# The int8 cross attention of a four-layer kernel, rewritten as a pipeline by ticks with engines in fixed order

## The chip, the cores and the metric

The kernel runs on one core of one Trainium2 chip. Its engines are TensorE (PE, with its weight loads shown as PEld), VectorE (DVE), ScalarE (ACT), GpSimd (POOL) and SyncE (SP), which issues most DMAs. The metric is the device time of one execution in microseconds; the median of several runs is given. A profile is one more execution, recorded by the hardware profiler.

## The reference, cut to what matters

The program computes four residual layers over x of 4 x 512 x 512: a cross attention with int8 fake quantisation, a mixture of experts, a second cross attention and a feed-forward. Only the first is touched. With 16 heads of 32 columns:

```python
def _qdq(x):
    s = jnp.maximum(jnp.max(jnp.abs(x), axis=-1, keepdims=True) / 127.0, 1e-08)
    return jnp.clip(jnp.round(x / s), -127.0, 127.0) * s
q = _qdq(x) @ _qdq(wq).T + bq
kv = cond @ wkv.T + bkv
k, v = jnp.split(kv, 2, axis=-1)          # then split into 16 heads
attn = jax.nn.softmax(jnp.einsum('bnhd,bmhd->bhnm', q, k) * scale, axis=-1)
o = jnp.einsum('bhnm,bmhd->bnhd', attn, v).reshape(B, N, C)
out = _qdq(o) @ _qdq(wp).T + bp

x = x + jnp.tanh(g_xattn[0]) * _L0_xattn_ref(_layernorm(x, axis=-1), ctx_2048, ...)
```

## The kernel before, in words

`xattn_int8` is the first stage. For each of 4 batches it goes through 4 groups of 4 heads (`oc`); a group is a unit of 16 score tiles, four heads by four tiles of 128 queries, each tile 128 queries by 512 keys. There are 256 score tiles in all.

For a score tile, `scores` multiplies query and key (PE, L438), takes the negated row maximum (DVE, L443) and the exponential with its row sums (ACT, L446). `turn`, two ticks later, transposes the tile in four pieces (PE, L460) and copies it from PSUM to the tile `a_pT` (`evac`, alternately DVE L120 and ACT L122). `weigh`, after every eight tiles, makes 16 small products with the values (PE, L468), each with 32 output columns, so that four heads stand beside each other in PSUM, and copies the result to `a_oT`. When a batch's four groups are done, `codes` turns 128 tokens back, divides by the sums and rounds them to int8 codes; `project` turns the codes, multiplies by `wp` (PE, L505), scales (DVE, L510), adds the bias (POOL, L511) and adds to x (DVE, L513).

The preparation of a batch (`prepare`) makes the values (PE L373, DVE L377), the layer norm and codes of x (L137 to L159), their turning (L382) and a row of scales (L165, L166). That of a unit (`heads`) makes the key (L403) and the query (L414, L419). `stacked` splits each into a high and a low half (ACT L334, DVE L335), so that a product of 4 x 32 rows sums high and low parts. It writes both halves to DRAM in one transfer (L339) and reads them back in four (L342), each of which fills 32 partitions for all four heads.

A product of plain f32 operands, as in L403, L373 and L468, stands in the trace as two matmul instructions with a weight load each; those of f32r (L438) and bf16 (L414, L505), and the transposes, as one.

The order comes from two places. `Line` puts steps behind each other: steps that are due in a tick, then `ceil(rest / ticks left)` preparation steps, each of which is a whole block of several engines' instructions (L199 to L205). The framework's scheduler may then reorder instructions between engines by their readiness. `Ordered` and `Beat` stand further down the file: `Ordered` keeps an engine's instructions in the order in which the program gives them (its calls all show as L567), `Beat` sorts steps by tick and by named place in the tick. The mixture of experts and the second attention use them already.

All PSUM is held by four pools of two banks each: `ps_m` for preparation and projection, `ps_s` for scores, `ps_t` for transposes, `ps_o` for weighing. `clear_slots` (L265) fills 39 slots in DRAM with zeros, which the mixture of experts needs later; it has the scheduler put them behind the loading of the next context.

Of the kernel before, what the change touches and what calls it, by code (L numbers as in the profile page):

```python
# [22 lines left out]
P = 128  # L23
# [46 lines left out]
class Kernel:  # L70
# [27 lines left out]
    def load_x(self, b):  # L98
        xv = self.a["x"].rearrange("(n p) d -> p n d", p=P)
        self.nc.sync.dma_start(self.x[:, ts(b, TB), :], xv[:, ts(b, TB), :])  # L100

# [7 lines left out]

    def spread(self, pool, name):  # L110

        v = pool.tile([P, D], F32, name=f"{name}_sb")
        self.nc.sync.dma_start(v, self.a[name].partition_broadcast(P))
        return v
# [70 lines left out]
class Line:  # L185

    def __init__(self):
        self.now, self.due, self.steps, self.ticks = 0, {}, [], 1  # L190

    def later(self, ticks, step):
        self.due.setdefault(self.now + ticks, []).append(step)

    def fill(self, steps, ticks):

        self.steps, self.ticks = list(steps), ticks

    def tick(self):  # L199
        for step in self.due.pop(self.now, []):  # L200
            step()
        for _ in range(-(-len(self.steps) // max(1, self.ticks))):
            self.steps.pop(0)()
        self.ticks -= 1
        self.now += 1  # L205

    def fill_all(self):
        while self.steps:
            self.steps.pop(0)()

    def drain(self):
        while self.due:
            self.tick()


def xattn_int8(k):

    nc, tc, a = k.nc, k.tc, k.a
    HG = KC
    with ExitStack() as ctx:
        wpool = ctx.enter_context(tc.tile_pool(name="a_w", bufs=1))
        p1 = ctx.enter_context(tc.tile_pool(name="a_1", bufs=1))
        p2 = ctx.enter_context(tc.tile_pool(name="a_2", bufs=2))
        p4 = ctx.enter_context(tc.tile_pool(name="a_4", bufs=4))
        p5 = ctx.enter_context(tc.tile_pool(name="a_5", bufs=5))  # L230
        p6 = ctx.enter_context(tc.tile_pool(name="a_6", bufs=6))
        dram = ctx.enter_context(
            tc.tile_pool(name="a_d", bufs=2, space=bass.MemoryType.DRAM)
        )
        ps_m = ctx.enter_context(tc.tile_pool(name="a_psm", bufs=2, space=PSUM))
        ps_s = ctx.enter_context(tc.tile_pool(name="a_pss", bufs=2, space=PSUM))
        ps_t = ctx.enter_context(tc.tile_pool(name="a_pst", bufs=2, space=PSUM))
        ps_o = ctx.enter_context(tc.tile_pool(name="a_pso", bufs=2, space=PSUM))
        scale = 1.0 / math.sqrt(DH0)

        wkvT = wpool.tile([P, KC, 2 * D], F32, name="wkvT")
        wkv = a["wkvT"].rearrange("(c p) o -> p c o", p=P)
        ctxTs = {}

        def load_ctx(b, chunks=((0, KC),)):
            ctxTs[b] = p1.tile([P, KC, S], F32, tag="a_ctxT", name=f"a_ctxT{b}")
            of = a["ctxT"][:, ts(b, S)].rearrange("(c p) t -> p c t", p=P)
            for c0, c1 in chunks:
                got = nc.sync.dma_start(ctxTs[b][:, c0:c1], of[:, c0:c1])
                if b == 0:  # L250
                    nc.sync.dma_start(wkvT[:, c0:c1, D : 2 * D], wkv[:, c0:c1, D : 2 * D])
            return got.ins


        load_ctx(0, [(c, c + 1) for c in range(KC)])
        bv = k.spread(wpool, "bv")
# [6 lines left out]
        def clear_slots(n, m, behind):  # L263
# [9 lines left out]
                ),  # L273
                reason="not needed early",
            )

        def coded_weight(name):


# [1752 lines left out]
```

## Time and profile before

| What | Value |
|---|---|
| median of 3 runs | 3576.08 us (3575.98 to 3579.71) |
| profiled execution, its own time | 3574.1 us |
| its span, first to last instruction | 3572.4 us |
| busy share of the span | PE 93%, DVE 61%, ACT 43%, POOL 38% |
| mean granted TensorE clock | 0.970 |
| first score of the first stage (L438) | at 61.7 us |
| last exponential of the first stage (L446) | at 602 us |
| last addition to x of the first stage (L513) | at 628.3 us |

A row of the groups or of the timeline names the line of the kernel, the engine and the operation, then the tiles as out<-in, the shape, and how many. Behind a bar or in brackets stands the idle time of the engine just before, and what ended it. A row of the waits reads: who waited, for whom, microseconds in total, how many times, the longest. Busy time of PE is a poor measure of its fullness, since matmuls are pipelined and the ends shown are modelled; the distance from one weight load to the next says more.

### The profile page before, as it was taken

What the parts mean: (1) busy time and instruction counts of PE and PEld (TensorE: products, weight loads), DVE (VectorE), ACT (ScalarE), POOL (GpSimd) and SP (SyncE); (2) the same over time, 40 slices, a digit from 0 to 9 for tenths busy, and PEclk for the clock granted to TensorE, in tenths of its full rate; (3) what the DMA queues carried; (4) which work ended last, traced back from release to release, by engine and by line L of the source; (5) the groups of instructions that cost most, each with busy time, mean ns of one, the idle gap of its engine ahead of it and who ended that gap; (6) DMA issues with size and microseconds to landing.
All of it is one profiled execution on the core that took longest, in us unless ns stands there. A gap on an engine that the chain in (4) does not pass through costs nothing.

```text
span 3572.4 us, 47015 instructions
## 1 busy us (share of the span) xinstructions
PE 3333.4 (93%) x15536; PEld 2190.3 (61%) x15552; DVE 2172.4 (61%) x4580; ACT 1544.1 (43%) x4456; POOL 1355.3 (38%) x1526
## 2 busy tenths in 40 slices
PE   6988987889999889989999999999999999999997
PEld 3544544534554444447777777776777777777775
DVE  6676767543133336525558766678766687676657
ACT  2544545111211223345554455554555554555543
POOL 1000000341000134624446654557545466544443
PEclk8999999899999999989999999999999999999998
DMA  5534441476354673552323233223332332333211
GB/s 183 156 98 130 121 101 41 167 254 234 104 198 151 225 257 128 177 174 72 115 98 107 101 115 110 95 99 108 109 125 92 118 107 77 128 105 111 83 60 36
DMA packets 223026, 452.86 MB, mean 127 GB/s; under 512 B 21440, under 2 KB 80320, under 8 KB 220224
## 3 DMA queue, kind: packets, MB, share of 16 engines
q1 hardware_dynamic: 206432, 412.62, 35.2%
q10 hardware_dynamic: 11232, 20.45, 1.7%
q0 software_dynamic: 5120, 16.78, 1.4%
q8 instruction: 125, 2.05, 0.2%
q14 instruction: 117, 0.96, 0.1%
HBM read 420.87 MB, written 116.98 MB: 151 GB/s over the span
## 4 chain that ended last, share of the span: by engine, by line
PE 73%; DVE 13%; DMA 4%; ACT 4%; POOL 3%; issue 3%; SPq 0%; DVEq 0%; POOLq 0%; ACTq 0%
PE ps_w L567 10%; PE pss L567 10%; PE ps_p L567 9%; PE ps_o L567 9%; PE ps_t L567 7%; PE m_pk L567 5%; PE po L888 3%; PE pu L870 3%; PE pw L870 3%; PE po L468 3%; PE pt L460 3%; DVE f_y L567 2%; PE pss L438 2%; PE pk L403 2%; PE pv L373 2%
## 5 line engine op out<-in xcount | busy, mean ns | idle before, releaser
L567 PEld LDWEIGHTS ps_w<-g_pT,g_v 128*128 128x128 f32 x2048 | 388.8, 191 | 299.7 <-issue 223.1
L567 ACT ACTIVATE g_p<-pss,nm 128x512 f32<-128x512 f32 x512 | 350.9, 685 | 479.7 <-DVE nm L567 436.4
L567 PE MATMUL ps_w<-g_pT,g_v 128*128 128x256 f32 x2048 | 530.4, 382 | 24.1 <-DVE f_y L567 13.7
L567 PE MATMUL pss<-g_kT,g_qT 128*128 128x512 f32 x1024 | 524.1, 594 | 0.9 <-ACT g_p L567 0.9
L567 POOL TENSOR_SCALAR g_p<-g_p,rs 128x512 f32<-128x512 f32 x512 | 368.4, 721 | 382.1 <-DVE rs L567 370.6
L567 DVE TENSOR_REDUCE nm<-pss 128x1 f32<-128x512 f32 x512 | 350.9, 685 | 102.7 <-PE pss L567 101.7
L567 PE MATMUL ps_t<-ident,g_p 128*128 128x128 f32 x2048 | 307.5, 273 | 0.0
L1142 POOL TENSOR_TENSOR hl<-raw,hl 128x512 fp32r<-128x512 f32 x80 | 102.0, 1282 | 519.2 <-ACT hl L1141 503.1
L567 POOL TENSOR_TENSOR g_rstd<-ss,neghalf 128x4 f32<-128x4 f32 (+1 forms) x192 | 185.0, 964 | 297.5 <-ACT ss L567 297.3
L567 PE MATMUL ps_p<-g_wq,g_xq 128*128 128x512 f32 x1024 | 282.3, 417 | 5.3 <-DMA g_wq<-s_q 4.9
L567 PE MATMUL ps_o<-g_wp,g_cq 128*128 128x512 f32 x1024 | 287.0, 423 | 0.0
L567 DVE COPY g_pT<-ps_t 128x512 f32<-128x512 f32 x244 | 167.1, 685 | 165.8 <-PE ps_t L567 165.4
L567 POOL TENSOR_TENSOR f_t<-f_y,f_c 128x512 f32<-128x512 bf16 (+1 forms) x180 | 206.6, 1148 | 155.4 <-DVE f_c L567 87.1
L567 PEld LDWEIGHTS ps_t<-ident,g_p 128*128 128x128 f32 x2048 | 243.8, 141 | 26.3 <-POOL g_p L567 1.1
L567 ACT COPY g_pT<-ps_t 128x512 f32<-128x512 f32 x268 | 156.1, 583 | 233.4 <-PE ps_t L567 233.4
L446 ACT ACTIVATE p<-pss,nm 128x512 f32<-128x512 f32 x256 | 175.3, 690 | 135.9 <-DVE nm L443 134.5
L567 PE MATMUL m_pk<-m_wx,m_ctxT 128*128 128x512 f32 x512 | 230.0, 592 | 0.0
L567 PEld LDWEIGHTS ps_o<-g_wp,g_cq 128*128 128x128 f32 x1024 | 196.7, 192 | 41.4
L567 PEld LDWEIGHTS ps_p<-g_wq,g_xq 128*128 128x128 f32 x1024 | 191.4, 190 | 48.9 <-issue 7.1
L443 DVE TENSOR_REDUCE nm<-pss 128x1 f32<-128x512 f32 x256 | 173.2, 687 | 70.7 <-PE pss L438 69.3
L567 ACT ACTIVATE junk<-ps_p 128x128 f32<-128x128 f32 x640 | 177.1, 277 | 68.5 <-PE ps_p L567 54.2
L567 DVE RECIPROCAL rs<-g_sm 128x1 f32<-128x1 f32 x512 | 82.5, 161 | 203.3 <-ACT g_p L567 201.4
(317 smaller groups left out, 6025.4 us busy)
## 6 DMA issues: line engine op xcount, KB each, us to landing
m_w<-in_w_dram SPq DMA_DIRECT2D x39, 1792.0 KB
g_wp<-s_proj SPq DMA_DIRECT2D x128, 512.0 KB
m_w<-in_w_dram SPq DMA_DIRECT2D x39, 896.0 KB
g_wq<-s_q SPq DMA_DIRECT2D x128, 256.0 KB
g_wq<-s_qx SPq DMA_DIRECT2D x128, 256.0 KB
st_k<-dhl_k SPq DMA_DIRECT2D x64, 256.0 KB
st_q<-dhl_q SPq DMA_DIRECT2D x64, 256.0 KB
s_proj<-hl SPq DMA_DIRECT2D x32, 512.0 KB
```

The source lines that it names most:

```text
L373: nc.tensor.matmul(pv, lhsT=ctxT[:, ic, ts(t, P)], rhs=wkvT[:, ic, D : 2 * D], start=(ic == 0), stop=(ic == KC - 1),)
L403: nc.tensor.matmul(pk, lhsT=wkvT[:, ic, ts(oc, P)], rhs=ctxT[:, ic, :], start=(ic == 0), stop=(ic == KC - 1),)
L438: nc.tensor.matmul(pss, lhsT=qk["q"][:, h, ts(qt, P)], rhs=qk["k"][:, h, :], start=True, stop=True,)
L443: nc.vector.tensor_reduce(nm, pss, AX.X, ALU.max, negate=True)
L446: nc.scalar.activation(p, pss, AF.Exp, bias=nm, accum_out=sums[:, qt, n : n + 1])
L460: nc.tensor.transpose(pt[:, c, :], p[:, ts(c, P)], k.ident)
L468: nc.tensor.matmul(po[ts(h, DH0)], lhsT=v[:, c, ts(oc * 4 + h, DH0)], rhs=pTs[h][:, c, :], start=(c == 0), stop=(c == TB - 1),)
L567: return lambda *args, **kw: self.tc.keep_in_program_order(call(*args, **kw))
L870: nc.tensor.matmul(pp, lhsT=work[:, 1, ts(c, P)], rhs=w[:, c, half, :], start=(c == 0), stop=(c == KC - 1),)
L888: nc.tensor.matmul(po, lhsT=work[:HC, 3, ts(m, P)], rhs=w[:, m, :], start=(m == 0), stop=(m == NHC - 1),)
L1142: nc.gpsimd.tensor_tensor(hl[:, 1, :], raw, hl[:, 0, :].bitcast(F32), ALU.subtract)
```

## The change

`Line`, `prepare`, `heads` and `stacked` go. `Ordered` and `Beat` move above `xattn_int8`, and every instruction of the stage but two small set-up ones goes through an `Ordered` engine, SyncE's transfers included.

A unit is 16 ticks, a tick is one score tile. Each step has its tick and its place in it; preparation and projection are cut into steps of one engine's work each: a product, or a copy, or a scaling in a tick. The weighing is two steps of 8 products each in two successive ticks per half unit. Copies out of PSUM go to DVE or ACT by a running account (`work`) of the microseconds given to each. A stack goes from SBUF to SBUF in 16 transfers, each of 32 partitions by 512 numbers (64 KB), without the way through DRAM. `ctxT` has two buffers instead of one, `ps_s` three banks instead of two, `ps_o` one instead of two, `a_pT` five buffers instead of six. The rounding of the weights' codes moves from DVE to POOL. Before the first tick x and `wq` are loaded first and three of the four value products stand last; the slots are cleared one in five ticks. The first and second token tiles of a batch are projected from ticks 0 and 1 of the next unit, the others from 8 and 9.

```diff
-            by_half = dram.tile([P, 2, S], F32, tag="a_dhl", name=f"dhl_{name}")
-            nc.sync.dma_start(by_half, hl.bitcast(F32))
-            made = p2.tile([P, 4, S], F32R, tag=f"a_{name[0]}4", name=f"st_{name}")
-            for r, half in enumerate(order):
-                nc.sync.dma_start(
-                    made[ts(r, DH0)].bitcast(F32),
-                    by_half[:, half, :].rearrange("(h p) s -> p h s", p=DH0),
-                )
...
+            def send(self):
+                self.made = made = p2.tile(
+                    [P, 4, S], F32R, tag=f"a_{self.name[0]}4", name=f"st_{self.name}"
+                )
+                for r, half in enumerate(self.order):
+                    for h in range(4):
+                        SY.dma_start(
+                            made[ts(r, DH0), h, :].bitcast(F32),
+                            self.hl[ts(h, DH0), half, :].bitcast(F32),
+                        )
...
+        def evac(out, in_, us):
+
+            if behind[VE] < behind[AE]:
+                work(VE, us)
+                VE.tensor_copy(out, in_)
+            else:
+                work(AE, us)
+                AE.copy(out, in_)
...
+            def code(self, oc):
+                GE.tensor_scalar(
+                    self.ws[oc], self.ws[oc], self.r[:, oc : oc + 1], MAGIC, ALU.mult, ALU.add
+                )
+                GE.tensor_scalar(
+                    self.codes[:, oc, :], self.ws[oc], -MAGIC, 1.0, ALU.add, ALU.mult
+                )
...
+            def plan(self, u):
+
+                at(u + 2, "project", self.multiply_query)
+                at(u + 3, "normal", self.scale_query)
+                at(u + 4, "squares", self.query)
+                at(u + 5, "normal", self.q.low)
+                at(u + 5, "load", self.q.send)
+                for ic, n in enumerate((0, 1, 5, 6)):
+                    at(u + n, "project", partial(self.multiply_key, ic))
+                at(u + 7, "squares", self.key)
+                at(u + 8, "normal", self.k.low)
+                at(u + 8, "load", self.k.send)
...
+            at(u, "begin", begin)
+            for half in range(2):
+                for h in range(4):
+                    for q in range(2):
+                        n = u + half * 8 + 2 * h + q
+                        score, turn, evacuate = scores(h, half * 2 + q)
+                        at(n, "scores", score)
+                        at(n + 2, "turn", turn)
+                        at(n + 3, "evacuate", evacuate)
+                part, evacuate = weigh(half)
+                n = u + half * 8 + 7
+                at(n + 4, "weigh", partial(part, 0))
+                at(n + 5, "weigh", partial(part, 2))
+                at(n + 6, "normal", evacuate)
...
+            at(m, "turn_in", turn_in)
+            at(m + 1, "normal", divide)
+            at(m + 2, "codes", code)
+            at(m + 3, "turn_in", turn)
+            at(m + 4, "turned", turned)
+            at(m + 5, "project", multiply)
+            at(m + 6, "normal", scaled)
+            at(m + 7, "codes", add)
...
+            u = b * HG * UNIT
+            for t, m in enumerate((0, 1, 8, 9)):
+                project(u + HG * UNIT + m, batch, t)
+            if b + 1 < B:
+                after = batches[b + 1]
+                at(u + 1, "load", partial(load_ctx, b + 1))
+                at(u + 7, "begin", after.begin)
+                for t in range(TB):
+                    n = u + t * UNIT
+                    for ic, m in enumerate((8, 9, 13, 14)):
+                        at(n + m, "project", partial(after.multiply_value, t, ic))
+                    at(n + 15, "normal", partial(after.value, t))
+                    n = u + 18 + 4 * t
+                    at(n, "codes", partial(after.stats, t))
+                    at(n + 1, "codes", partial(after.norm, t))
+                    at(n + 2, "codes", partial(after.code, t))
...
+        for n in range(SLOTS):
+            at(40 + 5 * n, "load", partial(clear_slot, n))
+        beat.run()
```

The places of a tick, in order: begin, gate, weighed, divide, evacuate, normal, turned, squares, gated, scores, weigh, project, turn_in, turn, rest, codes, load.

## The prediction

> **What bounds the kernel now.** I read first the windows view, to find the stage that the change touches, then the waits and the groups of that stage, then its timeline tick by tick, and last SyncE's queue. Columns of the windows view: stretch, its length, then busy time of PE, PEld, DVE, ACT and POOL, the granted clock, the DMA share and GB/s.
>
> ```profile
> 0.00:61.00 61.00, 33.87 (x95) 15.61 (x96) 33.94 (x87) 6.65 (x10) 7.53 (x17) 0.81 0.66 215
> 61.00:603.00 542.00, 469.65 (x2776) 269.94 (x2790) 379.35 (x675) 283.93 (x699) 26.08 (x31) 0.95 0.42 113
> 603.00:629.00 26.00, 11.82 (x67) 5.08 (x66) 18.04 (x45) 1.76 (x3) 6.12 (x12) 0.66 0.07 16
> 1600.00:3490.00 1890.00, 1859.96 (x9600) 1412.38 (x9600) 1280.49 (x2793) 989.88 (x3012) 1016.39 (x1161) 1.00 0.30 102
> 99.50:104.90 5.40, 5.40 (x28) 3.28 (x27) 3.77 (x7) 3.88 (x9) 0.00 (x0) 1.00 0.98 211
> ```
>
> The int8 attention is the first 629 us: 61 before the first score, 542 for 256 score tiles (2.11 us each), 26 after the last. The fourth row is the later attention, which already runs by `Beat` and `Ordered`: PE is idle for 30 of 1890 us there. The first stage has PE "busy" 470 of 542 us, but with matmuls whose ends are modelled and which wait on others:
>
> ```profile
> ACT p L446 <- DVE nm L443: 134.5, 65, 13.7
> DVE nm L443 <- PE pss L438: 69.3, 99, 6.9
> PEld pss L438 <- ACT p L446: 59.2, 81, 6.1
> ACT a_pT L122 <- PE pt L460: 52.8, 80, 2.3
> PEld pss L438 <- DMA st_q<-dhl_q: 10.3, 2, 10.1
> ```
>
> Each engine waits for another in a ring (PE for ACT, ACT for DVE, DVE for PE), with single waits up to 13.7 us: no engine is full, the order of the work is the bound. The timeline shows the price of a tick:
>
> ```profile
> 434.83 0.19 PEld L438 LDWEIGHTS pss<-st_k,st_q 128*128 128x128 f32 x1 [0.54 <-ACT p L446]
> 435.50 0.19 PEld L438 LDWEIGHTS pss<-st_k,st_q 128*128 128x128 f32 x1
> 435.64 0.57 PEld L460 LDWEIGHTS pt<-ident,p 128*128 128x128 f32 x4
> 436.45 0.14 PEld L468 LDWEIGHTS po<-a_pT,a_v 128*32 128x32 f32 x2 [0.24 <-ACT a_pT L122]
> 437.13 0.19 PEld L438 LDWEIGHTS pss<-st_k,st_q 128*128 128x128 f32 x1 [0.54 <-ACT p L446]
> ...
> 304.96 1.43 PEld L468 LDWEIGHTS po<-a_pT,a_v 128*32 128x32 f32 x26 [0.42 <-ACT a_pT L122]
> 306.81 0.30 PEld L403 LDWEIGHTS pk<-a_ctxT,wkvT 128*128 128x128 f32 x2 [0.41 <-issue]
> ```
>
> A tick of one score and four transposes needs 0.67 us of PE (434.83 to 435.50). A tick into which the scheduler has put two of the 32 weighing instructions takes 1.63 (435.50 to 437.13), and half a unit has three of those and a burst of 26 (1.85 us). So half a unit is about 3 x 1.6 + (0.7 + 2.1) + 4 x 0.7 = 10.4 us, 32 of them 333 us; the other 209 us is preparation and projection, put in as blocks between ticks, behind which score, max and exp stand idle.
>
> SyncE's queue:
>
> ```profile
> 95.70 0.34 SPq L339 DMA_DIRECT2D dhl_k<-hl_k  x1
> 98.59 1.73 SPq L342 DMA_DIRECT2D st_k<-dhl_k  x4
> ```
>
> A plain transfer takes 0.34 us to issue (0.38 with the gap); the four-part ones 0.43 (0.47 with the gap).
>
> **The change part by part.** A unit is 16 ticks.
>
> *PE.* The rows count instructions, and a product of plain f32 is two (L403 shows 112 for 14 units of 4 products). Fixed order gives the weighing as two parts of 16 instructions per half unit. The burst of 26 takes 1.85 with its end, so 16 take 1.2, plus 0.1 for entering: 1.3. Half a unit: 8 x 0.68 + 2 x 1.3 = 8.0 us instead of 10.4. Per unit 16.1, the next key 8 x 0.43 = 3.4 (0.43 is the distance of neighbouring loads of L403) and query 4 x 0.22 = 0.9: 20.4. Per batch: values 32 x 0.43 = 13.7, or 3.4 a unit; turning the codes and rows 2.7 in the third unit; projection 4 x (4 x 0.11 + 4 x 0.06 + 4 x 0.22) = 6.2 in the next batch's first. So a plain unit is 23.8 us of PE, the third 26.5, a first unit 30.0; the last batch, with nothing to prepare, 83.5 in all. The stage: 100.6 (first batch, with `wp`'s turning) + 2 x 104.1 + 83.5 = 392 us.
>
> *DVE* (start to start of neighbours: reduce or 512-wide f32 copy 0.60, the two-input form 0.66). Plain unit: 16 max x 0.60 = 9.6, query scaling and two lows 2.0, value 0.6: 12.2. Norm and codes of the next batch: 4 x 2.8 = 11, over the second and third unit. Projection 4 x 3.5 = 14, all in a batch's first unit: 26.2 there.
>
> *ACT.* Exp with its accumulator read is 0.67: 16 x 0.67 = 10.7, two highs 1.2: 11.9. The copies out of PSUM (16 x 0.48, two of 0.27, few others) go to the engine that the new `work` account has as less loaded, 9 to 10 us a unit. DVE and ACT together: 12.2 + 11.9 + 9.5 = 33.6, or 17 each. PE's 23.8 covers them in a plain unit; in a batch's first unit nearly all copies fall to ACT (21), and DVE's 26 lies close under PE's 30. Were PE faster, they would bound the loop at about 345.
>
> *SyncE.* The way through DRAM goes (5 issues and two landings for each stack); 16 issues of 64 KB come in, 32 a unit. The nearest row for such a plain transfer is L339's: 0.38 us; the four-part row (0.47) is the other end. They stand in one queue: query's 16 from tick 5, key's 16 behind them, and a slot clearing about every fifth tick (0.4 each), the loads of x and context too. PE's score at tick 16 needs, for its head, the key's first 13. The chain: five ticks at 1.55 = 7.8, copy, low and handover 1.2, 29 x 0.38 = 11.0, two clearings 0.8, landing 1.6 (2.9 us from 95.70 to 98.59 is the upper end, for eight times the bytes): 22.4 us. That is just under PE's 23.8; by the 0.47 row it is 25.0 and just over. So the transfers are what is late next, and behind a late score waits all of PE, since its order is now fixed.
>
> Against this stands a rule. In 99.50 to 104.90 one stack (1 MB in pieces of 32 partitions) kept all 16 engines 98% busy at 211 GB/s. The Trainium skill, page "SBUF — State Buffer", sections "Door 1: The DMA port swizzle" and "The DMA setup-cost knee", says that 32 partitions reach 8 of 16 ports, and that a loop of 64 KB transfers runs at about 138 GB/s: one large transfer, not several. By the rule 64 KB is 0.475 us, the chain 29 x 0.1 = 2.8 us longer, 25.2, at the edge of PE's time: some 15 us over the stage. By the row, 64 KB at 211 GB/s is 0.31, under the issue of 0.38. I take the row for the sum and the rule for the range.
>
> The loop: 392 us of PE, 257 for the tiles (333 before) and 135 for the rest (209 before, so some 75 of it was idle). The later attention holds PE at nearly its full issue, but with slack on DVE and ACT, which this stage has less of; and `ps_m` has two buffers, of which key holds one from tick 0 to 8, so that in a first unit each projection step waits for the other engine inside a tick. I take 0.94 of PE's issue, 417, and 8 for the three first units: 425 us instead of 541, or 1.66 a tick. At 0.98 it is 400, at 0.86 456. The `wp` rounding on POOL (0.72 an operation) is hidden under the first unit's ticks.
>
> *Start.* x and wq come first, then context with the key half. 4 MB at the 215 to 264 GB/s of the start is 17 us, DVE's norm and codes end by about 21 (they stood last in the old order), PE's key product (8 instructions, up to 0.86 each at the clock of 0.6 to 0.8 there) to 25; the key's 16 issues lie beside the turning of wq and x, to 34; then query, scaling, high, low, 16 x 0.38 = 6 and the landing: 45. Three value tiles (24 x 0.43 = 10 us) lie in PE's order before the first score, beside those transfers. I take 47 (40 to 57), against 61.7. *End.* Two token tiles project before the last unit is weighed, two after: weighing, copy, then one chain of about 10 us and 3 for the second: 14 instead of 27. Moving wq's rounding to POOL: 8 x 0.72 under the loads; without this cover it costs 6.
>
> Sum: 47 + 425 + 14 = 486 instead of 629, 143 less. The profiled execution took 3574.1 us (span 3572.4), 2 below the median of 3576.08, so 3431 for it and 3433 for the median. MoE and what follows do the same work.
>
> **The rivals.**
> 1. *The transfers pace every unit.* The chain is 11.4 + 29c. At c = 0.55 a plain unit is 27.4, 2 above my 25.3: over 13 units 27, in all 3460; at 0.65 30.3, in all 3498. For it: the rule, and issues of up to 1.96 us where a queue is full. Against: 0.34 for a plain issue.
> 2. *Lock step.* PE waits inside most ticks for DVE and DVE for PE (two `ps_m` buffers, the max behind the copy on DVE): a tick is 2.0 us, the loop 512, in all about 3520. For it: today's ring of waits. Against: two ticks lie between score and transpose, and there are three score banks.
> 3. *Slower: a transfer's landing holds the next issue.* Today's queue shows issues waiting for earlier transfers (clearings, 8.5 us in ten waits, 1.0 at most). If landings throttle the 512 small transfers, c grows; the break-even is (629 - 61) / 16 = 35.5 us a unit, c = 0.83. At 1.2 a unit is 46.2 and the time about 3747. Against: the 98% busy stretch moved 1 MB in 5.4 us, 0.34 per 64 KB, with DRAM as source; from SBUF to SBUF no row exists.
> 4. *No effect:* the fixed order is not what reaches the engines, or the gain is lost in later stages.
>
> **How the numbers follow.** My case 0.72 (3395 to 3470), rival 1 0.11, rival 2 0.09, rival 3 0.06, rival 4 0.02. Predicted 3433; the range 3385 to 3510 takes in my case with the bounds of start and loop, nearly all of rival 1 and the better half of rival 2. 0.2% of the time, 7 us, is about what a measurement can tell. Faster 0.92, same 0.02, slower 0.06.
>
> **What would show it.** After: first score near 47 us, last exp near 472, MoE's first turn near 486; weighing in groups of 16 instructions; PE busy without long gaps, its waits before a score the longest for st_k; SyncE's spacing 0.35 to 0.40. I am wrong if the spacing is over 0.5, if PE waits in most ticks for `ps_m`, or if a plain unit is over 28 us.

## The result, and the profile after

The changed kernel takes 3547.85 us (median of 4 runs, 3547.29 to 3548.41), beside 3576.48 for the kernel before (4 runs too): a ratio of 0.9922, 95% interval 0.9910 to 0.9934. It is faster by 28.6 us, a fifth of the 143 that were forecast, and outside the range. The profiled execution has a span of 3545.6 us.

The windows view of the kernel after, cut at its own stage borders: the score loop and the attention stage's tail. The columns are those of the windows shown before.

```profile
44.00:555.00 511.00, 419.24 (x2776) 257.24 (x2794) 355.80 (x656) 314.45 (x765) 36.39 (x51) 0.94 0.36 98
555.00:584.00 29.00, 13.05 (x84) 6.28 (x83) 19.64 (x44) 4.18 (x9) 6.43 (x12) 0.77 0.14 44
```

PE's busy time in the loop has fallen from 470 to 419 us, but the loop has only gone from 542 to 511: PE is now idle for 92 us of it. In 1890 us of the later attention PE's busy time is the same within 0.3 us. What PE waits for is in the waits view of the loop (43 to 560 us; engine, tile and line, what it waited for, us, times, longest):

```profile
ACT p L183 <- DVE nm L183: 180.0, 146, 11.5
DVE nm L183 <- PE pss L183: 85.0, 62, 6.6
PE pss L183 <- DMA st_k<-hl_k: 47.6, 12, 6.1
PEld pt L183 <- ACT a_pT L183: 27.5, 38, 1.6
PEld pss L183 <- DMA st_k<-hl_k: 12.4, 3, 6.3
```

Two links of the ring of waits are still there, and longer than before (the first two rows). The third, a score that waits for an exponential, has gone from 59.2 us to 3.7 (view of the tile `pss`); there are three score banks now. And a new wait has come: at 12 of the 15 changes of unit the first score waits for the key's stack, 47.6 us in PE's row, up to 6.1 at once. (PEld's row counts three of the same 12 waits again. The expectations below add both rows: 59.9 us in 15.) The other three changes, where no score waits, follow the long first units of batches 2 to 4. The timeline of SyncE's queue in the second batch's third unit says why the stack is late:

```profile
253.05 10.51 SPq L183 DMA_DIRECT2D st_q<-hl_q  x16
263.66 10.25 SPq L183 DMA_DIRECT2D st_k<-hl_k  x16
```

The sixteen issues of a stack take 10.3 to 10.5 us. The key's begin 0.1 us after the query's have ended; the thirteenth of them, the last that the next unit's first head needs, ends about 272.0, and PE's timeline has that unit's first score:

```profile
273.56 0.47 PE L183 MATMUL pss<-st_k,st_q 128*128 128x512 f32 x1 [1.38 <-DMA st_k<-hl_k]
```

The unit before it began at 243.7, so it lasted 29.9 us. The view of the tile `st_k` gives one issue (ns: least, median, most):

```profile
L183 SPq DMA_DIRECT2D st_k<-hl_k x240: 507/589/1739, 66.0 to 532.2; - x120
```

From start to start they are 0.633 us apart (median), where the forecast had 0.38.

A slow clock goes with the waits. In the loop the granted clock of PE falls to 0.50 in 11 stretches, 58 us together, and ten of these stand at the ten longest of the 12 waits. The windows view around the wait that ends at 500.6 us:

```profile
494.00:499.20 5.20, 0.71 (x5) 0.42 (x4) 1.74 (x3) 2.09 (x7) 0.00 (x0) 1.00 0.44 106
499.20:506.10 6.90, 5.51 (x12) 3.05 (x13) 1.98 (x3) 1.56 (x4) 0.00 (x0) 0.51 0.37 117
```

PE first has almost nothing to do, and then begins the new unit at half clock. That is where the loop's mean of 0.94 comes from. In the runs below in which the waits are short (2.4 us at most), 24 us (`a_early`) and 7 us (`a_ord_best`) of the loop are at 0.50. No run set the clock by itself, so that the waits bring the slow clock about is read from this coincidence alone.

In first units, with projections, something else holds the scores up. The timeline of ScalarE and VectorE near the start of the third batch:

```profile
306.95 0.68 DVE L183 TENSOR_TENSOR o<-pt_o,a_rs 128x512 f32<-128x512 f32 x1
307.66 0.69 DVE L183 TENSOR_REDUCE o_am<-o 128x1 f32<-128x512 f32 x1
...
308.26 0.68 DVE L183 TENSOR_REDUCE nm<-pss 128x1 f32<-128x512 f32 x1
...
308.98 0.69 ACT L183 ACTIVATE p<-pss,nm 128x512 f32<-128x512 f32 x1 [4.49 <-DVE nm L183]
```

The score behind this maximum was written by 306.8, but on VectorE a division and its maximum for the projection stand ahead of it, and ScalarE has nothing for 4.49 us. (Up to 308.1 us this stretch, too, has a granted clock of 0.50.) The tail, after the last exponential:

```profile
564.30 1.61 DVE L183 SCALAR_TENSOR_TENSOR y<-pp,o_s,sp_row 128x512 f32<-128x512 f32 x2 [3.07 <-PE pp L183]
...
566.50 1.73 DVE L183 SCALAR_TENSOR_TENSOR x_res<-y,tg,x_res 128x512 f32<-128x512 f32 x1 [0.59 <-POOL y L183]
...
568.89 0.68 DVE L183 TENSOR_TENSOR o<-pt_o,a_rs 128x512 f32<-128x512 f32 x1
...
574.14 0.61 PE L183 MATMUL pt_c<-identb,a_oc 128*128 128x128 bf16 x4 [7.52 <-DVE o_s L183]
```

The division for tokens 2 and 3 (568.89) stands in VectorE's order behind the sums of tokens 0 and 1, which wait for PE and GpSimd; PE then waits 7.5 us. The granted clock of the tail is 0.77.

Where the time went, by the borders of the stages (us):

| part | before | forecast | after | after less forecast |
|---|---|---|---|---|
| to the first score | 61.8 | 47 | 43.9 | -3 |
| first score to last exponential | 540.5 | 425 | 511.2 | +86 |
| to the last token sum (MoE's first normalised tile) | 27 | 14 | 28.4 | +14 |
| from there to attention 2's first score | 966.5 | 966.5 | 986.5 | +20 |
| from there to the end | 1976.6 | 1976.6 | 1975.6 | -1 |

The fourth row is a surprise: the text of the expert stage is the same in both kernels. Its copies out of PSUM have changed engines, which the view of the tile `m_work` in its expert slots shows; first the kernel before, then after:

```profile
L122 ACT COPY m_work<-pt x38: 577/586/587, 883.2 to 1295.8; 112x512 f32<-112x512 f32 x38
L120 DVE COPY m_work<-pt x38: 680/692/693, 883.6 to 1309.5; 128x512 f32<-128x512 f32 x37, 112x512 f32<-112x512 f32 x1
```

```profile
L110 DVE COPY m_work<-pt x38: 679/686/692, 842.8 to 1273.1; 112x512 f32<-112x512 f32 x38
L112 ACT COPY m_work<-pt x38: 579/585/587, 843.1 to 1285.4; 128x512 f32<-128x512 f32 x37, 112x512 f32<-112x512 f32 x1
```

The 112-row tile (hidden values, on the way from the up to the down product) was copied by ScalarE and is now copied by VectorE; the 128-row tile the other way round. `Kernel.evac` alternates by a counter, `self.flip`, while the program is built. The old attention stage calls it 333 times, an odd number; the new one has its own `evac` and never calls it.

### The profile page after: what moved, and what is told of

It is laid out like the page before. It is cut to its first block, busy times and chain, and to the rows that moved or that the text cites. A ratio compares the mean times of both kernels' runs of the same rounds, so it can differ in the third digit from the quotient of the medians.

```text
span 3545.6 us, 47829 instructions
## 1 busy us (share of the span) xinstructions
PE 3276.7 (92%) x15533; PEld 2174.2 (61%) x15552; DVE 2132.3 (60%) x4526; ACT 1578.6 (45%) x4530; POOL 1366.3 (39%) x1554
## 4 chain that ended last, share of the span: by engine, by line
PE 57%; DVE 8%; issue 3%; POOL 2%; DMA 2%; ACT 1%; SPq 0%; DVEq 0%; POOLq 0%; ACTq 0%
PE ps_w L183 10%; PE pss L183 10%; PE ps_p L183 10%; PE ps_o L183 9%; PE ps_t L183 8%; PE m_pk L183 5%; PE po L1062 2%; DVE f_y L183 2%; PE pu L1044 2%; PE pw L1044 1%; DVE nm L183 1%; DMA raw<-in_w_proj_dram 1%; DVE t_work L183 1%; DVE g_hn L183 1%; POOL hl L1316 1%
## 5 line engine op out<-in xcount | busy, mean ns | idle before, releaser
L183 PEld LDWEIGHTS pt<-ident,p 128*128 128x128 f32 x1024 | 124.1, 145 | 102.5 <-issue 56.3
```

What stands on the lines that cost most here:

```text
L183: return lambda *args, **kw: self.tc.keep_in_program_order(call(*args, **kw))
```

## Experiments

Each run's ratio is to runs of the kernel before that were made beside it (medians 3574 to 3578 us), so the ratios are the safer comparison. "Loop" is first score to last exponential, 511.2 us in the changed kernel. The next run has the same attention stage, and its loop is 513.1: a difference of 2 us in the loop says nothing.

### The alternation's counter

```diff
             at(40 + 5 * n, "load", partial(clear_slot, n))
         beat.run()
+        k.flip ^= 1
```

> The changed kernel with one line more: at the end of the attention stage the two-valued counter by which the shared copy-out helper alternates between VectorE and ScalarE is toggled once. The old attention stage called that helper an odd number of times (333 by the loops), the new one never calls it, so the expert stage begins with the other engine: in the trace before, the copy of a slot's turned rows is DVE's and that of the turned hidden values is ACT's; after, they have changed places. Theory: that swap is why the expert stage, whose text is the same, is 20.0 us longer (966.5 before, 986.5 after, from the last attention-1 write to the first score of attention 2). Then this run gives back 17 to 23 us, 3527 us (3524 to 3532), and the stage is 966 to 970 us. Rival: the stage is longer for another reason (addresses of its buffers, the order of the slots' clearing, what is in flight when it starts): then the time is 3545 to 3550 and the stage stays at 985 or so.

Measured: 3532.4 us, ratio 0.9874 (0.9860 to 0.9889), 15 to 17 us below the changed kernel. The stage is 968.4 us long (585.3 to 1553.8), and the 112-row copy is ScalarE's again.

The mirror image, the same line at the entry of `moe` in the kernel before:

> The kernel before, with the same counter toggled once at the entry of the expert stage, and nothing else. Theory of the swapped copies: the expert stage grows from 966.5 to about 986 us and the whole from 3576.5 to 3594 to 3599 us, with nothing of the attention pipeline in it. Rival (something else that the new attention stage leaves behind): 3575 to 3579 us.

Measured: 3592.08 us, ratio 1.0043 (1.0030 to 1.0056), and a stage of 984.2 us. So the swap is the cause of nearly all of the stage's 20 us: 18 by the length of the stage in both directions, 14 to 17 by the whole time, a little under what was expected. How it costs nearly 0.5 us a slot (the copy itself is 0.1 us longer on VectorE) was not taken apart.

### The transfers' way

Through DRAM again, under the new ticks and in the fixed order (the pool for the buffer in DRAM, which the edit adds too, is left out here):

```diff
-                for r, half in enumerate(self.order):
-                    for h in range(4):
-                        SY.dma_start(
-                            made[ts(r, DH0), h, :].bitcast(F32),
-                            self.hl[ts(h, DH0), half, :].bitcast(F32),
-                        )
+                by_half = dram.tile([P, 2, S], F32, tag="a_dhl", name=f"dhl_{self.name}")
+                SY.dma_start(by_half, self.hl.bitcast(F32))
+                for r, half in enumerate(self.order):
+                    SY.dma_start(
+                        made[ts(r, DH0)].bitcast(F32),
+                        by_half[:, half, :].rearrange("(h p) s -> p h s", p=DH0),
+                    )
```

> The changed kernel with the old way of stacking: each stack by one write to DRAM and four reads (10 transfers per unit instead of 32), ticks and fixed order as they are. Theory 1 (SyncE's issues set when the stacks are ready: 16 of them 0.63 us apart, so that the query stack takes 10.1 us and the key stack, issued behind it, is 10 us behind): the key stack is issued in about 2 us, needs two landings one after the other instead of one, and is still ready some 5 us sooner; the score's wait for the key stack (59.9 us in 15 waits) falls under 20 us, units with no preparation beside the projections' go from 29 to 32 us to 25 to 27, and the whole to 3480 to 3515 us. Theory 2 (the units are long because PE, VectorE and ScalarE wait for each other in the fixed order, and the key's wait only takes up slack): loop within 10 us of now, 3535 to 3550 us. Rival to both (DRAM's two landings are late as well): the wait stays near 60 us, and the time at 3545 to 3560 us.

Measured: 3552.71 us, ratio 0.9927 (0.9915 to 0.9939), the same as the changed kernel. The rival held: PE idles before the first score at the same 12 changes of unit, 46.5 us together, where it was 47.6. (The rows of the waits view hide this. They put only 16.1 us down to `st_k`, and 17.5 to `slots_in`, which no score reads; a wait there must be another transfer's.) SyncE's queue in the third unit of the second batch, as above:

```profile
261.83 1.17 SPq L183 DMA_DIRECT2D dhl_k<-hl_k  x1
268.56 1.73 SPq L183 DMA_DIRECT2D st_k<-dhl_k  x4
```

The key's issues now take 3 us, but its reads start 5.6 us after the write's issue has ended, because they need what it wrote. The last ends at 270.3, and the next unit's first score comes 5.4 us later; in the changed kernel it came 1.5 us after the last issue that it needs. Two quite different costs, sixteen issues or a second landing, end at the same tick; that this run moved nothing does not acquit the transfers. It only shows that this substitute was no faster.

The transfers alone, in the old order:

```diff
-            nc.sync.dma_start(by_half, hl.bitcast(F32))
...
             for r, half in enumerate(order):
-                nc.sync.dma_start(
-                    made[ts(r, DH0)].bitcast(F32),
-                    by_half[:, half, :].rearrange("(h p) s -> p h s", p=DH0),
-                )
+                for h in range(4):
+                    nc.sync.dma_start(
+                        made[ts(r, DH0), h, :].bitcast(F32),
+                        hl[ts(h, DH0), half, :].bitcast(F32),
+                    )
```

> The kernel before with only its transfers changed: each stack in 16 transfers from SBUF to SBUF, no DRAM buffer; order, ticks and pools as before. Theory 1: the two ways deliver a stack in about the same time (in the run with DRAM under the new ticks the time was the same within 5 us), so the transfers alone are worth within 8 us: 3570 to 3585 us. Rival: in the old order the stacks are prepared further ahead, both waits are hidden, and the shorter first unit (one landing instead of two) gives 5 us: 3568 to 3574 us. Other rival: SyncE with 32 issues of 0.63 us in a unit delays the loads that share it, and it is 10 to 40 us slower.

Measured: 3568.74 us, ratio 0.9978 (0.9969 to 0.9988), where its first rival had it. In the old order the transfers are worth 8 us by themselves; the first score comes at 57.6 instead of 61.8, and the loop is 536.3 instead of 540.5 (units of 26 to 30 us, one of 42, and one of 59 to 60 at the end of each of the first three batches). What the change brought beyond that belongs to its other parts together (ticks, order, banks, buffers, the account of the copies), less the counter's loss; of these only the order and some ticks and banks were tried below.

The same bytes by twice as many transfers:

```diff
                     for h in range(4):
-                        SY.dma_start(
-                            made[ts(r, DH0), h, :].bitcast(F32),
-                            self.hl[ts(h, DH0), half, :].bitcast(F32),
-                        )
+                        for c in range(2):
+                            SY.dma_start(
+                                made[ts(r, DH0), h, ts(c, S // 2)].bitcast(F32),
+                                self.hl[ts(h, DH0), half, ts(c, S // 2)].bitcast(F32),
+                            )
```

> The changed kernel with each of the 32 transfers of a unit cut into two of half the columns: the same bytes by twice as many transfers. If an issue costs SyncE its 0.59 us whatever it moves, a stack takes 20 us to issue, the key stack is ready 20 us later than now, and a unit is bound by 64 issues of 0.63, 40 us: 14 or so units 8 to 11 us longer each, 3660 to 3720 us. If the price goes with the bytes or the rows of a transfer (the issue of a half one takes 0.3 us), the time stays at 3545 to 3565 us. If the units are long for the lock step alone, and SyncE has slack, also under 3565.

Measured: 3839.33 us, ratio 1.0730 (1.0714 to 1.0745), worse than any theory had it. In SyncE's queue:

```profile
300.50 20.13 SPq L183 DMA_DIRECT2D st_k<-hl_k  x32
```

A transfer of 32 KB costs the queue the same 0.63 us as one of 64 KB: between these two sizes the price is the issue's, not the bytes'. Units last 49 to 54 us, not the 40 of a queue that is merely full. They are close to what the prediction's chain says: 11.4 + 29c becomes 11.4 + 58c with twice the issues, 48.1 us at c = 0.633. The expectation had counted the queue's work and left out that it begins only in the unit's fifth tick.

### When the stacks are prepared, and by which queue

```diff
-                    groups[g + 1].plan(u)
+                    groups[g + 1].plan(u - 2 if g % HG else u)
```

> The changed kernel with the preparation of the next unit's stacks two ticks earlier in the second, third and fourth unit of every batch (it begins in the last two ticks of the unit before); in the first units, where projections stand, it stays. The sends, their number and the fixed order stay. Theory 1 (what ends a plain unit is the chain: the query stack's sum ready about 9 us into the unit, 16 issues of it, then 16 of the key's, 20.8 us in all, then a landing): the chain begins two ticks, 3.3 us, earlier, so each of the waits for the key stack (59.9 us in 15 waits) loses about that: 10 or 11 of them, 30 to 37 us, 3508 to 3522 us. Theory 2 (lock step of the engines; the wait takes up slack that would be lost elsewhere): the wait moves to other rows, 3538 to 3550 us. Rival (SyncE is full and cannot begin earlier, since it is behind with its other transfers): no change either, and then SyncE's own waits for the query's sum stay under 140 us.

Measured: 3514.86 us, ratio 0.9826 (0.9812 to 0.9839), 33 us less, in the range of theory 1; the loop is 481.7 us. But by batches the gain is 15.1, 3.2, 0.8 and 10.3 us. In the first batch PE's waits at the changes of unit fell by 15 us and the batch by as much. In the two middle ones they fell by 16 us and the time by 4 alone. There PE's waits moved for the larger part, as theory 2 had it, to the copies of the transposed tiles. PE's rows of the waits view in the two middle batches, first of the changed kernel, then of this run:

```profile
PE pt L183 <- ACT a_pT L183: 4.2, 6, 1.3
PE po L183 <- ACT a_pT L183: 1.2, 3, 0.4
```

```profile
PE pt L183 <- ACT a_pT L183: 9.5, 8, 3.4
PE po L183 <- ACT a_pT L183: 5.9, 8, 1.1
```

Some of the gain is the clock's: 24 us of the loop at 0.50 instead of 58. Half of the difference, 17 us, is an estimate from these figures of the most that it can be.

The query's sixteen issues on GpSimd's queue instead, everything else as changed:

```diff
-                        SY.dma_start(
+                        (GE if self.name[0] == "q" else SY).dma_start(
```

> The changed kernel with the 16 transfers of the query stack issued by GpSimd, those of the key stack by SyncE as now. Theory 1 (the key's 16 issues stand behind the query's on one queue): the key's begin when its sum is ready, 3 to 4 us sooner in a plain unit, and the wait of 59.9 us falls to 10 to 30: 3505 to 3530 us. Against it: an issue on GpSimd costs about 1 us by the trace (its indirect transfers 1.02 us), 16 of them 16 us, and if that is what sets the query stack's time, the query is the late one by some 2 us and the gain is near nothing, 3540 to 3555 us. Theory 2 (lock step): 3538 to 3550 us.

Measured: 3516.79 us, ratio 0.9841 (0.9824 to 0.9858), 31 us less; the waits for `st_k` fall to 1.2 us and the loop to 480.6, though the first score comes at 49.7 us instead of 43.9. The guess of 1 us an issue on GpSimd was wrong: 0.50. One cost is visible in the timeline of GpSimd:

```profile
220.91 7.86 POOL L183 DMA_DIRECT2D st_q<-hl_q  x16 [2.76 <-ACT hl_q L183]
228.78 0.56 POOL L183 TENSOR_TENSOR ln_rstd<-ve,neghalf 128x1 f32<-128x1 f32 x1
```

A power of one column, for the normalisation that VectorE needs next, stands behind the sixteen issues; VectorE waits for it in the second unit of a batch, where a tick takes 6 us (units of 31 us).

The Trainium skill, page "DMA: Bandwidth & Descriptors", section "Issuing engines are not separate DMA queues", says that issuing from several engines saves only the sequencer's time for the issue, "which is usually small relative to the DMA itself". Here that time was the one that counted: 16 x 0.63 us, against one landing of 2.0 us (median of `st_q` in this run).

### Projections and banks

```diff
-            for t, m in enumerate((0, 1, 8, 9)):
+            for t, m in enumerate((0, 4, 8, 12) if b + 1 < B else (0, 1, 5, 6)):
```

> The changed kernel with the projections of a finished batch placed further apart: in the first unit of the next batch at ticks 0, 4, 8, 12 in place of 0, 1, 8, 9, and after the last batch at 0, 1, 5, 6. Number and kind of instructions are the same. Theory 2a (in ticks 0 to 6 and 8 to 14 of a first unit two projections one tick apart put two divisions with their maxima, 1.4 us each, and two codings, 1.3 us, on VectorE ahead of the next score's maximum, and PE, in fixed order, waits): one projection at a time leaves 1 to 2 us a tick, and the first units of batches 2 to 4 come from 39.3, 41.3 and 36.5 us to 33 to 36: 10 to 18 us; in the tail the divisions of tokens 2 and 3 no longer stand behind two sums that wait for PE: 2 to 5 us of its 28.4. Together 3525 to 3536 us. Theory 2b (it is the two product banks: each projection needs three of them, one after the other, while the key's product holds one for seven ticks): the same work still goes through one bank, and the first units stay within 2 us of now, 3540 to 3550 us.

Measured: 3535.31 us, ratio 0.9891 (0.9876 to 0.9906), against 0.9922: 11 to 13 us less by the medians, of which its profiled execution (span 3540.7) shows only 5. In that one the first units of batches 2 to 4 are 36.6, 36.9 and 34.6 us (39.3, 41.3, 36.5 before the edit), 9 less together, and the tail is 25.5 instead of 28.4. But the loop is only 2 us shorter: the wait for the key stayed (56.8 us by both rows, 59.9 before) and other units grew. Theory 2a holds for the places that it named; that the transfers kept the loop from collecting it is borne out by the run with all three edits below. Where the other 7 us of the median come from stays open.

```diff
-        ps_m = ctx.enter_context(tc.tile_pool(name="a_psm", bufs=2, space=PSUM))
-        ps_s = ctx.enter_context(tc.tile_pool(name="a_pss", bufs=3, space=PSUM))
+        ps_m = ctx.enter_context(tc.tile_pool(name="a_psm", bufs=3, space=PSUM))
+        ps_s = ctx.enter_context(tc.tile_pool(name="a_pss", bufs=2, space=PSUM))
```

> The changed kernel with one bank of PSUM moved from the scores (three to two) to the products (two to three). Theory 2b (first units are bound by the two product banks): the first units of batches 2 to 4 fall from 39 to 34 to 36 us, the units without projections rise by nothing to 2 us, as a score may start only when the one two before it is read; the whole 3535 to 3548 us. Theory 2a (VectorE's order in the tick, whatever the banks): first units as now or longer, plain ticks longer where the exponential of two scores before is late, 3550 to 3580 us.

Measured: 3543.05 us, ratio 0.9914 (0.9901 to 0.9928). The interval overlaps that of the change, so it tells little: first units of 37.1, 37.0 and 36.9 us, a new row of waits of `pss` for ScalarE's exponential (58.7 us in 96; 3.7 before), and a loop of 510.7. The third product bank takes 6 us off the three first units, less than theory 2b had (34 to 36 each), and scores with two banks wait for exponentials again.

### The fixed order

The ticks kept, the fixed order dropped for all engines:

```diff
-    VE, AE, GE, PE, SY = (
-        Ordered(tc, e) for e in (nc.vector, nc.scalar, nc.gpsimd, nc.tensor, nc.sync)
-    )
+    VE, AE, GE, PE, SY = nc.vector, nc.scalar, nc.gpsimd, nc.tensor, nc.sync
```

> The changed kernel with the ticks as they are, but its instructions of the attention stage given to the scheduler without the fixed order. Theory 2 (in the first units of a batch, 36.5 to 41.3 us long, PE and VectorE wait for each other because each must keep the written order): those units come down to 33 or so, the tail from 28 to about 20 us, and the whole to 3515 to 3535 us. Rival: the written order is what a scheduler would choose or better, and it goes back towards the old pattern of two long units in four: 3550 to 3600 us.

Measured: 3510.09 us, ratio 0.9809 (0.9794 to 0.9824): the fixed order costs this kernel 38 us. The first units of batches 2 to 4 came to 34.4, 35.9 and 29.4 us, about as theory 2 had it, and the tail to 23.9. The other units of the first three batches were not helped (28 to 33 us), and for another reason than before. The last batch was: its later units came from 30.4, 31.8 and 22.8 us to 24.3, 23.6 and 18.1, and with its first unit it holds 26 of the 35 us that the loop lost. In the first three batches the starts of the scores show 15 of them in 16 to 22 us and then 10 to 15 us to the next unit, and the expectation of the run after this one read that as a wait for the key's stack. It is not one: the tile `pss` has no wait for `st_k` in this run, and PE is busy in the two middle batches for 238 of 251 us. PE runs the scores ahead and does the turning and weighing later. The windows view of `po` alone in those batches, without fixed order, and below it in the fixed order (of the run `a_ord_best` below), has 512 weighing instructions each:

```profile
177.00:428.00 251.00, 56.14 (x512) 18.83 (x512) 1.70 (x4) 4.46 (x12) 0.98 0.36 99
```

```profile
160.00:404.00 244.00, 40.58 (x512) 14.75 (x512) 0.85 (x2) 5.27 (x14) 0.99 0.39 106
```

The scheduler puts the weighing in pieces again (2, 10, 16, 4 or 26 instructions in PE's timeline), and the same instructions occupy PE for 16 us longer, as far as modelled ends can say.

Without fixed order, with the counter set right and the preparation four ticks earlier (`plan(u - 4 if g % HG else u)`):

> The changed kernel without the fixed order in the attention stage (alone: 38 us less; its units then run their first 15 scores in 15 to 20 us and wait 10 to 15 us at the unit's end for the key stack), with the toggled counter, and the stacks prepared four ticks earlier in the second to fourth units. Theory 1 (without the fixed order it is still the chain of 32 issues and a landing that ends a unit): the chain begins about 6 us sooner, the units without projections fall from 28 to 33 us to PE's own work, 24 to 27: 11 units by 4 to 5 us. With 16 for the counter, 3438 to 3460 us. Rival (the scheduler takes the preparation when it likes, and the written ticks move nothing): 3490 to 3496 us.

Measured: 3490.89 us, ratio 0.9767 (0.9753 to 0.9780). This is the rival's number: after the counter's 16 us, next to nothing is left for the earlier preparation, since no score was waiting for a stack.

### Together, and whose order it is

In the fixed order, with the counter, the earlier preparation by two ticks, and the projections apart:

> The changed kernel, in its fixed order, with three edits together: the toggled counter (measured alone: 16 us less), the stacks prepared two ticks earlier in the second to fourth units (33 us less), the projections apart as in the run beside it (theory 2a: 12 to 22 us less). If the three are separate terms of the time, the sum is 3477 to 3490 us. If the last is nothing (theory 2b), 3497 to 3502.

Measured: 3479.5 us, ratio 0.9742 (0.9728 to 0.9755). The sum of the three single gains, 3477 to 3490, was met. In the loop they are not quite separate. Edit by edit it goes 511.2, 481.7 (earlier preparation), 469.1 (projections too): with the key's wait gone, spreading the projections is worth 12.6 us of loop, where alone it gave 2. It is in the first units: those of batches 2 to 4 come from 40.5, 40.4 and 37.4 us to 35.9, 35.9 and 32.8.

Then the same with one side freed. PE's order kept, the other four engines left to the scheduler, by these lines in place of the one that orders all five:

```diff
+    VE, AE, GE, SY = nc.vector, nc.scalar, nc.gpsimd, nc.sync
+    PE = Ordered(tc, nc.tensor)
```

> The version with the three edits (toggled counter, preparation two ticks earlier, projections apart; 3479.5 us), with the fixed order kept for PE's instructions alone; VectorE, ScalarE, GpSimd and SyncE take the scheduler's. If the waits left are the order of VectorE and ScalarE (a copy or a maximum behind work that is not needed yet), PE's busy time stays at 216 of some 230 us in the middle batches, and the whole is 3455 to 3472 us. If PE's own order in the tick is what makes it wait (it asks for a transposed tile before the copy can be done), the scheduler can gain nothing beside a fixed PE: 3474 to 3485 us.

Measured: 3461.83 us, ratio 0.9684 (0.9671 to 0.9698), the fastest of all, 3.2% below the kernel before. And the reverse, PE left to the scheduler and the other four in fixed order:

> The same version with PE's instructions given to the scheduler, and the other four engines in the fixed order. If PE's own order makes it wait, it can now run scores ahead and defer the weighing: 3455 to 3472 us. If what a free PE order costs is the mixing of kinds of product (without any fixed order PE was busy 238 us for what takes 216 in fixed order), PE's busy time in the middle batches rises from 216 to 230 or more, and the whole is 3480 to 3505 us.

Measured: 3507.1 us, ratio 0.9808 (0.9794 to 0.9823). The middle batches in the windows view, first `a_pe_only`, then `a_pe_free`:

```profile
154.20:383.80 229.60, 210.45 (x1457) 128.66 (x1457) 180.52 (x345) 163.25 (x393) 18.53 (x22) 0.99 0.42 118
```

```profile
172.00:430.70 258.70, 241.11 (x1456) 133.09 (x1456) 189.83 (x363) 160.93 (x393) 19.95 (x26) 1.00 0.36 98
```

Both went the way expected, the second 2 us beyond its range. With its own order fixed PE is busy for 216 us of two batches (`a_ord_best`) or 210, and for 241 without. The weighing makes up most of that: the view of `po` in these windows gives 40.6 and 35.5 us, and 61.3 without. Fixing the others' order gains nothing here and costs 23 us of loop: ScalarE's wait for `nm` is 137.0 us in the loop with all fixed and 87.5 with PE's alone. Which of the four engines matters was not separated.

## Why the prediction was wrong, point by point

- **Start, 47 forecast, 43.9 measured.** In its range, with luck: two terms missed in opposite directions. The key's product had ended by 18.8 us (forecast 25), and the 32 issues of the two stacks took 24.7 us (9 and 6 forecast).
- **Weighing in groups, 392 us of PE.** Right as far as the runs show. Groups of 16 are in the timeline, and PE's busy time in the two middle batches fell from 254.8 to 217.7 us, 23 of it in the weighing (60.6 to 37.4). Once the other obstacles are out (`a_pe_only`), the two middle batches last 114.4 and 115.2 us, beside the 113.4 that the prediction's sum gives for each (104.1 / 0.94 and 2.7 for a first unit). First and last batch are 113.1 and 103.7 there (forecast 107 and 91.5); why those two are longer was not tried.
- **The issue, c = 0.38. This is the first step that failed: a mis-sized term, which measured 0.633.** The chain itself, 11.4 + 29c, was right: at 0.633 it gives 29.8 us for a plain unit, and those of batches 2 and 3 measured 28.6 to 31.9. So rival 1 was the case, given 0.11, though not alone: at 0.65 it had 3498 us for the whole. The row chosen, a transfer from SBUF to DRAM, differed in two ways. It has no second end in SBUF; no row of the old trace has. And it stands alone in its queue. An issue right behind another takes longer, and the old trace showed that: a slot clearing took 0.320 us alone and mostly 0.42 to 0.46 right behind another issue. The clearings, whose text is the same but for their place, show it again, first in the kernel before, then after, where most stand behind a stack or behind each other:

```profile
L265 SPq DMA_DIRECT2D slots_in<-zero x39: 319/320/1286, 122.0 to 427.0; - x39
```

```profile
L183 SPq DMA_DIRECT2D slots_in<-zero x39: 320/577/1636, 141.9 to 522.1; - x39
```

The estimate of 0.475 us for 64 KB, worked out from the 138 GB/s of the Trainium skill (page "SBUF — State Buffer", section "The DMA setup-cost knee"), erred to the same side. Taken as a rate it makes the cost go with the bytes, and the halved transfers show that here it went with the number of issues. The upper end of this cost should have been set well above the two figures at hand.

- **"0.94 of PE's issue, and 8 for the three first units."** The second. Rival 2, lock step, was partly true: the written order of the four engines beside PE adds about 23 us to the loop (469.1 to 446.4 when freed), and projections in pairs 13. In the middle batches it stood right behind the transfers, as the earlier preparation showed. The three first units were 39.3, 41.3 and 36.5, 13 us above the 34.6 each that the forecast's figures give. The prediction took the later attention as its measure, but there DVE and ACT have slack, which it said itself. (Its bound of 345 us by DVE and ACT does not follow from the figures beside it; shared evenly they come to some 310.) The rivals had been treated as one or the other; they were both there, and the transfers hid a part of the lock step. The sum also puts the clock at nothing: PE's costs are those of ticks at full clock, while the prediction's own row gave 0.95 for the loop before; after, it was 0.94, and 0.99 in `a_ord_best`.
- **End, 14 forecast, 28.4 measured.** The chain of one projection was counted on an engine that has nothing else to do. In the written order, VectorE does tokens 0 and 1 to their last sum before it divides for tokens 2 and 3. Moving two of the ticks took off 2 to 3 us (28.4 to 25.5, and 25.5 to 23.4 in the pair with the earlier preparation); 24 remain with PE's order alone. What the rest is was not separated.
- **"MoE and what follows do the same work."** The same work, but on other engines: 20 us lost, 18 of them by the counter. It was readable in the code: the diff takes the last calls of a helper with a state out of one stage, while a later stage uses it.

Of the loop's excess of 86 us, 30 go with the earlier preparation (with the slow clock that followed the waits), 13 with the projections' places once that is done, 23 with the freed order of the other four engines, and 21 stay (18 of them in the first and last batch). The split holds for this order of the edits; the projections' places alone gave 2.

## What to carry to other kernels

Cost a transfer by a row with the same two memories, the same partitions and the same place in its queue, alone or behind another; where there is none, take its issue as unknown, since a serial chain multiplies it by its length (29 here). Here it paid to fix the order of the engine that is the bound and whose instructions cost more when mixed, and to leave the engines with slack to the scheduler. Look at a gain batch by batch before calling a wait its cause: the same edit gave 15 us in one batch and 1 in another. And when code is removed, look for state that it leaves behind while the program is built: a flip-flop in a helper moved 16 us into a stage that nobody had touched.

## What the runs showed of the hardware

What an issue costs SyncE's queue depends on the transfer and on what stands right ahead of it. One of a stack, from SBUF to SBUF, takes 0.51 us when the queue is idle before it and 0.589 right behind another (0.633 from start to start), at 64 KB and at 32 KB alike. A slot clearing, from SBUF to DRAM, takes 0.320 when the queue is idle, 0.457 behind another clearing and 0.580 right behind an issue of a stack (medians in the kernels before and after). A four-part read from DRAM takes 0.43 behind another. GpSimd issues a stack's transfer in 0.496. What makes the issue of a stack dearer, the two ends in SBUF or the 32 partitions, no run separates.

Around the end of PE's ten longest waits for a stack in the changed kernel (2.8 to 6.1 us) its granted clock was at 0.50 for 3 to 7 us; at the two of 1.4 and 2.7 us it was not.
